# Who issues the four loads of block 0's A: ScalarE and SyncE, or SyncE alone

## The chip, the core and the metric

The kernel runs on one core of one Trainium2 chip. The metric is the device time of one execution in microseconds (us). The time before is the median of five runs, 474.98 us (474.37 to 475.48).

## The reference, cut to what matters

```python
# x (8, 256, 1024); A (8, 1024, 16); B (8, 16, 1024); one adapter number of 3..7 for each of 8 batches
Bx  = einsum('bni,bri->bnr', x, B[ids])          # rank 16
c   = einsum('bnr,bor->bno', Bx, A[ids])         # back to 1024
q   = fp8(clip(c / in_scale))                    # rounded to float8_e4m3
hid = silu(q @ gate_w.T) * (q @ up_w.T)          # 2752 wide, with scales
out = x + fp8(hid) @ down_w.T                    # with scales
```

So each batch picks a small adapter (B, then A) by its number, the result is rounded to fp8, and a feed-forward layer of 1024 to 2752 to 1024 follows, with x added at the end.

## The kernel before, in words

**Tiling.** The 8 batches of 256 tokens are four blocks (t = 0 to 3) of 512 tokens, two batches each. 1024 features are 8 slices of 128 (k). The 2752 hidden features are 22 slices of 128 (c), the last one half full. Everything is held transposed: features on partitions, tokens along the free dimension.

**Stages.** For block 0: `two_times_b` (L562) multiplies x by the two adapters' B into `bx`; VectorE and ScalarE copy it to `bm` (L578); `two_times_a` (L626) multiplies `bm` by A into `c`, 64 small products; VectorE and ScalarE round `c` to fp8 as `xg` (L614, L616). Then `gate_up(c, t)` (L686) makes 16 products of 128x512 for a slice c, and hid from them. The first `NFIRST` = 5 slices are done for block 0 alone (L762 to L771), then block 1's adapter stage (`two_times_b_in_parts`, `two_times_a_parts`) comes in the middle of slice 4, and so on to blocks 2 and 3. From slice 5 on, each weight tile serves all four blocks. Last come the products with the down weights (`yd`). A second path (`general`) is taken only for inputs that are out of bounds here; it does not run.

**Products of zeros.** `pass_time` (L527) issues products of a tile of zeros on TensorE at three places: 16 of 128x512 ahead of `two_times_b`, 4 of 128x128 between its k = 6 and k = 7, 7 of 128x128 between its end and `two_times_a` (L757 to L761). TensorE's order is written out by hand (`tc.keep_in_program_order`), so these stand where they stand whether data is there or not.

**Loads and their queues.** Nearly all loads are issued by SyncE, in program order, on one hardware queue (q1 in the profile). At the start ScalarE issues a few on its own queue (q10): the adapter numbers `ids_i`, the B of block 0's first batch, and two loads of block 0's A. A load of A or B needs its batch's adapter number in a register of the engine that issues it; `adapter_of` (L374) reads it there (`value_load`: a load from `ids_i`, register operations and a check, L375).

`a_two[0]` holds block 0's A as four groups of 16 rows. `load_a_two(t, j, adapter, queue)` (L382) loads the two groups g = 0, 1 of batch j, 32 KB each; the products of `two_times_a` read partitions 32q to 32q + 31, with q = 2g + j, in the order q = 0, 1, 2, 3. Thus "first" (j = 0) is read by q = 0 and 2, "second" (j = 1) by q = 1 and 3. The tile is filled with zeros by GpSimd before (L370).

The order of the loads at the start, as the program stands: x of block 0 in four pieces (k = 0-1, 2-4, 5-6, 7: 512, 768, 512 and 256 KB; L398), the two Bs (68 KB each; L378), the four As (L385), then the gate and up weights of slices 0 (two halves of 512 KB) and 1 to 4 (1 MB each; L408), six reads of adapter numbers, the Bs of block 1, x of block 1 in three pieces, its four As (`a_twice`, L391), x of block 2, and on.

**Eight completion semaphores.** The order of the built program shows that transfers take eight completion semaphores in turn, whichever engine issues them, and that an issue waits until the transfer that had its semaphore before has landed:

| semaphore | 0 | 1 | 2 | 3 | 4 | 5 | 6 | 7 |
|---|---|---|---|---|---|---|---|---|
| before, first turn | ids | x 0-1 | x 2-4 | B first | A first g0 (ScalarE) | A first g1 (ScalarE) | B second | x 5-6 |
| before, second turn | x 7 | A second g0 | A second g1 | w 0, half 0 | w 0, half 1 | w 1 | w 2 | w 3 |
| before, third turn | w 4 | B of block 1 | B of block 1 | x of block 1 | x of block 1 | x of block 1 | a_twice | a_twice |

So, for example, A second g1 waits for x 2-4, and w 1 waits for A first g1.

Of the kernel before, what the change touches and what calls it, by code (L numbers as in the profile page):

```python
# [284 lines left out]
def adaln_ffn(  # L285
# [15 lines left out]
    nc = tc.nc  # L301
# [48 lines left out]
    with ExitStack() as fast:  # L350
# [23 lines left out]
        def adapter_of(batch, queue):  # L374
            return queue.value_load(ids_i[0:1, batch : batch + 1], min_val=0, max_val=7)  # L375
# [6 lines left out]
        def load_a_two(t, j, adapter, queue=nc.sync):  # L382
            for g in range(2):
                row = 32 * (2 * g + j) + R * j
                queue.dma_start(  # L385
                    out=a_two[t][row : row + R],
                    in_=a8[bass.ds(adapter * 2 * R + g * R, R), :],
                )
# [6 lines left out]
        def load_x(t, k):  # L395
            piece, first = x_of(x4, t, k)
            ks = slice(first, first + piece.shape[1])
            nc.sync.dma_start(out=xs[t][:, ks, :], in_=piece)  # L398
# [16 lines left out]
        first, second = adapter_of(0, nc.scalar), adapter_of(1, nc.sync)  # L415
        load_b(b_two[0], 0, first, nc.scalar)
        load_b(b_two[0], 1, second, nc.sync)
        load_x(0, 5)
        load_a_two(0, 0, first, nc.scalar)
        load_x(0, 7)  # L420
        load_a_two(0, 1, second, nc.sync)
        for c in range(NFIRST):
            load_gate_up(c, parts=1 if c else 2)
        adapters = [adapter_of(2 + q, nc.sync) for q in range(6)]
# [434 lines left out]
        for k in range(NH - 1):  # L859
# [23 lines left out]
            first = k % 2 == 0  # L883
# [133 lines left out]
```

## Time and profile before

| | |
|---|---|
| median of five runs | 474.98 us |
| the profiled execution: time, span | 475.39 us, 473.6 us |
| TensorE busy | 468.6 us (99% of the span), 2482 products |
| VectorE, ScalarE, GpSimd busy | 107.0, 193.6, 11.5 us |
| DMA, mean over the span | 114 GB/s, 53.84 MB |
| DMA in the first 40 us | 370 GB/s, 14.78 MB |
| the two As issued by ScalarE | at 3.46 and 3.99 us, 3.9 and 4.8 us to landing |
| the two As issued by SyncE | at 4.51 and 6.06 us, 4.8 and 3.4 us to landing |

Times on a page of the profile count from the span's start. A row of the timeline is: start, duration from the first to the last end of the merged group, engine, line, operation, output<-inputs, count, and in brackets the idle time just before it with what ended it. PE is TensorE, PEld its weight loads, DVE VectorE, ACT ScalarE, POOL GpSimd; SPq and ACTq are the sequencers of SyncE and ScalarE, where a DMA_DIRECT2D is the issue of a transfer and not the transfer. The time to landing counts from the start of the issue. The chain of waits is followed back from the last instruction: at each step, what released it.

### The profile page before, as it was taken

Reading aid. Unit: us, or ns where it says so; the run is one execution under the profiler, and the core shown is the slowest. Engines: PE = TensorE matmul, PEld = TensorE weight load, DVE = VectorE, ACT = ScalarE, POOL = GpSimd, SP = SyncE. Lnnn points to the kernel's source line nnn. Section 1 sums busy time; section 2 is a strip of 40 time slices with the busy share of each in tenths; the row PEclk is TensorE's granted clock in tenths of the full one; section 3 lists DMA queues with packets and bytes.
Section 4 is the critical chain, followed back from the end, with each engine's and each line's share of the span. In section 5 each row is a group of like instructions: output and inputs, shape, how many; then the busy total and the mean of one; then the engine's idle time right before and its main releaser. Section 6 shows DMA issues by size and latency. Waiting matters only on the chain.

```text
span 473.6 us, 5982 instructions
## 1 busy us (share of the span) xinstructions
PE 468.6 (99%) x2482; PEld 215.8 (46%) x2482; DVE 107.0 (23%) x169; ACT 193.6 (41%) x253; POOL 11.5 (2%) x26
## 2 busy tenths in 40 slices
PE   9999999999999999999999999999999999999997
PEld 5444544444444444444444444444444444444444
DVE  1342621212122121212212121232120121031031
ACT  1342538995555645443354544359212022021000
POOL 0022300000000000000000000000000000000000
PEclk9999999999999999999999999999999999999999
DMA  8997023322222112222211111233335245163031
GB/s 312 412 381 220 1 88 120 148 90 89 90 89 90 61 34 84 89 90 89 90 62 35 37 62 57 61 101 106 110 141 161 71 179 162 28 215 108 3 115 68
DMA packets 15060, 53.84 MB, mean 114 GB/s; under 512 B 1778, under 2 KB 3058, under 8 KB 12978
## 3 DMA queue, kind: packets, MB, share of 16 engines
q1 hardware_dynamic: 14816, 53.25, 32.8%
q8 instruction: 21, 0.34, 0.3%
q10 hardware_dynamic: 210, 0.14, 0.1%
q14 instruction: 13, 0.11, 0.1%
HBM read 44.99 MB, written 8.39 MB: 113 GB/s over the span
## 4 chain that ended last, share of the span: by engine, by line
PE 92%; DMA 5%; ACT 0%; ACTq 0%; SPq 0%; DVE 0%; issue 0%; DVEq 0%
PE y L525 59%; PE yd L525 32%; DMA w_gu<-w_gu 3%; DMA a<-a_twice 2%; DMA a<-a 1%; PE c L525 1%; PE bx L525 1%; SPq L408 0%; ACT L310 0%; ACT xg L616 0%; ACTq L385 0%; ACTq L309 0%; ACTq L378 0%; DVE a_parts L454 0%; DVE a_parts L455 0%
## 5 line engine op out<-in xcount | busy, mean ns | idle before, releaser
L525 PE MATMUL y<-xg,w_gu 128*128 128x512 fp8e4 x1376 | 298.0, 379 | 0.2 <-ACT xg L616 0.2
L525 PEld LDWEIGHTS <-w_gu 128*128 128x128 bf16 x1376 | 134.2, 98 | 162.2 <-issue 0.6
L525 PE MATMUL yd<-hid,w_d 128*128 128x512 fp8e4 (+2 forms) x693 | 146.0, 373 | 0.0
L704 ACT ACTIVATE g<-y,gate_s 128x512 f32<-128x512 f32 (+1 forms) x88 | 59.7, 682 | 140.8 <-PE y L525 140.8
L733 DVE SCALAR_TENSOR_TENSOR hid<-y,up_by_down,g 128x512 fp8e4<-128x512 f32 x84 | 63.0, 751 | 217.2 <-PE y L525 154.0
L525 PEld LDWEIGHTS <-w_d 128*128 128x128 bf16 x693 | 66.6, 98 | 78.9 <-issue 1.7
L511 ACT ACTIVATE junk<-w_d 128x1408 bf16<-128x1408 uint16 (+1 forms) x16 | 21.2, 1323 | 88.3 <-DMA w_d<-w_d 88.2
L824 DVE SCALAR_TENSOR_TENSOR o<-yd,down_s,x 128x512 f32<-128x512 f32 x28 | 20.0, 746 | 107.5 <-PE yd L525 93.6
L511 ACT ACTIVATE junk<-w_gu 128x2048 bf16<-128x2048 uint16 (+1 forms) x22 | 41.0, 1863 | 0.0
L518 ACT ACTIVATE junk<-hid 128x2048 bf16<-128x2048 fp8e4 x21 | 40.0, 1906 | 0.5
L518 ACT ACTIVATE junk<-xg 128x2048 bf16<-128x2048 fp8e4 x8 | 15.3, 1909 | 0.3
L614 DVE TENSOR_SCALAR xg<-c,inv 128x512 fp8e4<-128x512 f32 (+1 forms) x17 | 11.0, 712 | 4.4 <-PE c L525 4.3
L616 ACT ACTIVATE xg<-c,inv 128x512 fp8e4<-128x512 f32 (+1 forms) x17 | 9.8, 664 | 2.3 <-PE c L525 2.3
L525 PE MATMUL warm<-zeros 128*128 128x512 bf16 (+1 forms) x27 | 7.1, 429 | 1.2 <-DVE zeros L312 1.2
L824 DVE SCALAR_TENSOR_TENSOR o<-yd,down_s,xg 128x512 f32<-128x512 f32 (+2 forms) x5 | 3.2, 644 | 12.3 <-PE yd L525 9.8
L525 PEld LDWEIGHTS <-zeros 128*128 128x128 bf16 x27 | 2.8, 123 | 5.1 <-issue 3.7
L511 ACT ACTIVATION_READ_ACCUMULATOR junk<-w_gu 128x1 f32 x22 | 4.2, 192 | 0.0
L525 PE MATMUL yd<-hid_tail,w_dt 64*128 64x512 bf16 (+1 forms) x32 | 4.1, 377 | 0.0
L733 DVE SCALAR_TENSOR_TENSOR tail<-y,up_by_down,g 64x512 fp8e4<-64x512 f32 x4 | 3.0, 756 | 4.9 <-ACT g L704 4.8
L518 ACT ACTIVATION_READ_ACCUMULATOR junk<-hid 128x1 f32 x21 | 3.9, 187 | 0.0
L525 PE MATMUL bx<-x,b_four_twice 128*32 128x256 f32 x64 | 3.7, 380 | 0.0
L578 ACT COPY bm<-bx 64x128 f32<-64x128 f32 x2 | 0.5, 262 | 7.2 <-PE bx L525 7.2
(69 smaller groups left out, 56.0 us busy)
## 6 DMA issues: line engine op xcount, KB each, us to landing
w_gu<-w_gu SPq DMA_DIRECT2D x13, 1024.0 KB, 4.8
w_gu<-w_gu SPq DMA_DIRECT2D x17, 512.0 KB, 4.1
outT<-o SPq DMA_DIRECT2D x31, 256.0 KB, 2.2
w_d<-w_d SPq DMA_DIRECT2D x8, 704.0 KB, 5.0
w_d<-w_d SPq DMA_DIRECT2D x8, 640.0 KB, 3.9
x<-x SPq DMA_DIRECT2D x2, 2048.0 KB, 12.4
x<-x SPq DMA_DIRECT2D x2, 768.0 KB, 9.2
x<-x SPq DMA_DIRECT2D x2, 512.0 KB, 4.0
```

The costliest lines, as they stand in the source:

```text
L511: nc.scalar.activation(junk_like(w), low(w), AF.Copy, accum_out=lows[:rows, column : column + 1])
L518: nc.scalar.activation(junk_like(q), q, AF.Square, accum_out=squares[:rows, column : column + 1])
L525: tc.keep_in_program_order(nc.tensor.matmul(*args, **kwargs))
L578: copy(bm[64 * to : 64 * (to + 1), other], bx[half][64 * half : 64 * (half + 1)],)
L614: nc.vector.tensor_scalar(to, c, scale, None, ALU.mult, saturate=False)
L616: nc.scalar.activation(to, c, AF.Copy, scale=scale, saturate=False)
L704: nc.scalar.activation(g[rows], gates, AF.Silu, scale=gate_s[: gates.shape[0]])
L733: nc.vector.scalar_tensor_tensor(to, in0=ups, scalar=up_by_down[rows], in1=g[rows], op0=ALU.mult, op1=ALU.mult, saturate=False,)
L824: nc.vector.scalar_tensor_tensor(o, in0=y, scalar=down_s, in1=x, op0=ALU.mult, op1=ALU.add)
```

## The change

```diff
         load_b(b_two[0], 0, first, nc.scalar)
         load_b(b_two[0], 1, second, nc.sync)
         load_x(0, 5)
-        load_a_two(0, 0, first, nc.scalar)
         load_x(0, 7)
-        load_a_two(0, 1, second, nc.sync)
+        load_a_two(0, 1, second)
+        load_a_two(0, 0, adapter_of(0, nc.sync))
         for c in range(NFIRST):
             load_gate_up(c, parts=1 if c else 2)
```

`load_a_two`'s default queue is SyncE's. ScalarE no longer issues any A. SyncE issues, behind the last piece of x (k = 7): A second g0, A second g1, a read of batch 0's adapter number into a register of SyncE's own, A first g0, A first g1; then the weights as before. ScalarE still reads the number of batch 0 for its load of B.

In the built program the order of the instructions on TensorE, VectorE, ScalarE and GpSimd is the same but for ScalarE's two issues. The semaphores of the first transfers change:

| semaphore | 0 | 1 | 2 | 3 | 4 | 5 | 6 | 7 |
|---|---|---|---|---|---|---|---|---|
| after, first turn | ids | x 0-1 | x 2-4 | B first | B second | x 5-6 | x 7 | A second g0 |
| after, second turn | A second g1 | A first g0 | A first g1 | w 0, half 0 | w 0, half 1 | w 1 | w 2 | w 3 |

From w 0 on, every transfer has the semaphore that it had before.

## The prediction

> **What bounds the kernel now.** I read the page's busy times and chain first, then the chain in order of time up to 57 us, then the timeline of the first 35 us, then the stretches of DMA.
>
> ```profile
> span 473.6 us, 5982 instructions
> PE 468.6 (99%) x2482; PEld 215.8 (46%) x2482; DVE 107.0 (23%) x169; ACT 193.6 (41%) x253; POOL 11.5 (2%) x26
> ...
> PE 92%; DMA 5%; ACT 0%; ACTq 0%; SPq 0%; DVE 0%; issue 0%; DVEq 0%
> ```
>
> TensorE is the bound nearly throughout. The 5% of DMA in the chain all stand in the first 32 us:
>
> ```profile
> 3.99 4.82 DMA a<-a
> ...
> 10.27 12.97 DMA w_gu<-w_gu
> ...
> 23.79 7.47 DMA a<-a_twice
> ...
> 31.35 0.29 DVE rest L600
> 31.67 0.48 DVE a_parts L454
> 32.17 0.43 DVE a_parts L455
> 32.61 0.14 issue
> 32.74 0.75 PE c L525 x16
> ```
>
> The first of these rows is one of the loads that the change moves. But the chain gets from it to the next only over SyncE's issues: weights 1 wait for that A's semaphore, and weights 4 are issued behind them. Whether that costs time depends on whether the DMA engines run out of work meanwhile. After 34.4 us the chain is TensorE alone. So the change can matter in two ways: through block 0's `c`, which needs all four As, or through the arrival of block 1's data at 30 to 31 us.
>
> ```profile
> 4.51 1.87 SPq L385 DMA_DIRECT2D a<-a  x2
> 6.43 4.29 SPq L408 DMA_DIRECT2D w_gu<-w_gu  x6
> 9.63 0.56 PE L525 MATMUL warm<-zeros 128*128 128x128 bf16 x7
> 9.73 0.60 DVE L578 COPY bm<-bx 64x128 f32<-64x128 f32 x2 [2.62 <-PE bx L525]
> 10.13 2.17 PE L525 MATMUL c<-bm,a 32*128 32x128 f32 x64
> 14.36 0.98 SPq L378 DMA_DIRECT2D b<-b  x2
> 29.45 1.23 PE L525 MATMUL bx<-x,b_twice 128*32 128x128 f32 x32 [0.48 <-DMA x<-x]
> 32.74 0.51 PE L525 MATMUL c<-bm_parts,a_parts 32*128 32x256 f32 x8 [0.23 <-DVE a_parts L455]
> ```
>
> Here one sees that `c` starts at 10.13 right behind the zeros (no idle time in its row), that the last A landed at 6.06 + 3.4 = 9.46, so 0.67 us earlier, and that TensorE has idle time only in block 1's stage: 0.48, then about 0.15 inside the group of 1.23 (its twin ahead of it took 1.08), then 0.23: 0.86 us together.
>
> **What the change does, part by part.**
>
> *ScalarE* loses two issues (3.46 to 4.32 us). Its next work is the copy to `bm` at 9.79, which waits for `bx`. Worth nothing: the wait of 7.22 us in front of that copy takes it all up.
>
> *SyncE* gets two issues and a read of a number. From the rows: x 7 is issued at 3.81 and A second g0 at 4.51, both as before (its old wait for x 0-1, landed at 0.73 + 3.3 = 4.03, was over). Two As in a row on ScalarE stand 0.53 us apart (3.46, 3.99), so A second g1 goes at 5.04 and ends at 5.38; its old wait for x 2-4 (to 6.06) is gone. The read costs 0.58: between the last issue of weights (6.43 + 4.29 = 10.72) and the issue at 14.36 stand six of them and 0.13 of register work. Then 0.19 of register work (0.53 less an issue of 0.34): A first g0 at 6.15, A first g1 at 6.68, both with their semaphores free (x 2-4 landed at 6.06). Weights 0, half 0, follow at 7.05 instead of 6.43: **0.62 us later**. Half 1 at 7.51 (7.41 before, as it waited for A first g0). Weights 1 wait for x 5-6, landed at 3.31 + 4.8 = 8.11, so 8.11 instead of 8.82; weights 2 to 4 follow about 0.3 to 0.7 earlier than their 9.19, 9.67 and 10.27, unless x 7 or the As hold them.
>
> *DMA.* Is there work while half 0 is 0.62 late? The stretches (span, busy engines, clock, share, GB/s):
>
> ```profile
> 0.00:2.00 2.00, 0.82 (x2) 0.28 (x3) 0.43 (x6) 0.71 (x1) 1.13 (x8) 1.00 0.17 25
> 2.00:4.00 2.00, 2.00 (x6) 0.76 (x5) 0.00 (x0) 0.57 (x1) 0.00 (x0) 1.00 0.90 354
> 4.00:6.00 2.00, 2.00 (x6) 0.76 (x5) 0.00 (x0) 0.00 (x0) 0.00 (x0) 1.00 1.02 380
> 6.00:7.00 1.00, 1.00 (x6) 0.34 (x4) 0.61 (x8) 0.00 (x0) 0.00 (x0) 1.00 1.03 366
> 7.00:8.00 1.00, 1.00 (x30) 0.72 (x32) 0.11 (x1) 0.00 (x0) 0.00 (x0) 1.00 1.00 363
> ```
>
> By 8.00 us 50 + 708 + 760 + 366 + 363 = 2247 thousand bytes had moved. Ahead of half 0 stand x (2048 KB), two Bs (136 KB) and four As (128 KB), 2312 KB or 2367 thousand bytes, the same in both kernels. So 120 thousand bytes are left at 8.00, 0.33 us at 363 GB/s: work until 8.33. The first x, issued at 0.73, shows its first bytes in the quarter from 1.50, some 0.9 us later (my estimate from those rows). Half 0 issued at 7.05 is thus there from about 7.95, 0.38 us before the queue runs dry. I price the late issue at nothing, covered by the queue of x and A. If the cover is gone, all later transfers shift by at most the 0.62, and with them block 1's data and the end: bounds 0 and 0.62. On the other side, earlier issues of weights can close the dip at 8 to 9 us (309 GB/s against 410 in the next microsecond, about 0.25 us), and no more. From then on the queue is full (a mean of 370 GB/s over 40 us) and serves the same bytes in the same order, whatever the issue times. I take 0, the nearest row being the queue itself.
>
> The Trainium skill ("DMA: Bandwidth & Descriptors", section "Issuing engines are not separate DMA queues") says that issuing from several engines saves only the sequencer's time, as all run on the same DMA engines. That speaks against this change by the sequencer's 0.62 us and by nothing else; taken as lost it would give the 0.62 above.
>
> *The As and `c`.* The last A is issued at 6.68 instead of 6.06. In the rows, SyncE's A of 4.51 landed at 9.31 and that of 6.06 at 9.46: 1.55 us between the issues, 0.15 between the landings. They land when the queue has come to them, behind x 7, not a fixed time after the issue. The bytes ahead are the same. Bounds: 6.68 + 3.4 = 10.08 by the shortest of the four rows, 6.68 + 4.8 = 11.48 by the longest; by the queue 9.46 to 9.6. I take 9.6, as the nearest row is an A behind the same x. `c` needs it at 10.13 (q = 2 is the third product): 0.5 us to spare, and even the shortest row's 10.08 is in time. No wait is added on the path. When the weights' half 0 lands later than its 6.43 + 4.1 = 10.53, by 0.62 at worst, that is 11.15, and `gate_up` reads it at 12.26.
>
> Sum against the profiled execution: 475.39 + 0 = 475.39. It lies 0.41 above the median of the five runs, so the forecast in terms of the median is **474.98, rounded 475.0**.
>
> **Rivals.**
>
> *A becomes the bound (slower).* The point is where the last A lands. Up to 10.13 nothing. Up to 10.13 + 0.86 = 10.99 TensorE's block 0 shifts, but block 1's stage waits for DMA anyway and gives it back. Beyond, it counts one to one: at the upper bound 11.48 about 0.5 us, 475.5. It would be slower by over 0.2% from a landing of 11.94, 5.3 us after the issue, longer than any of the four rows; or if the gap also slows TensorE. The first products of zeros have their weight loads 0.43 us apart from 1.58 to 6.28 (2.01, 2.44, 2.86), while 72 products of the same width at 12.26 take 15.7 us, 0.218 each: at the start TensorE runs at half speed for some 5.1 us. Falling back to that for as long would cost 2.55 us, so up to 478.1. Against it: after the idle 0.48 at 29 us the products keep their usual 379 ns. The skill ("TensorE: Matmul & The Clock Gate", section "Part 1: The HAM clock gate") puts the fall at an idle window of about 3.4 us; by that a gap of 1.3 us costs no clock.
>
> *The queue runs dry.* Half 0's first bytes come later than 8.33. For it: the dip to 309 GB/s shows that the queue was thin there. At most 0.62: 475.6, still within 0.2%.
>
> *Block 1's data comes earlier (faster).* By the dip, up to 0.25: 474.7. However early it came, TensorE can gain only its idle 0.86 (474.1), which is under 0.2%; more would need something that no row shows.
>
> *The change does not do what it says:* the order of the built program shows all four As on SyncE, so no chance is given.
>
> **How the numbers follow.** 0.2% (0.95 us) is about what a measurement of this kernel tells from no change. Hidden, at 475.0, own range 474.4 to 475.6: 0.72. Queue dry: 0.08, all within 0.2%. A bound: 0.13, of it 0.11 slower by over 0.2% and 0.02 within. Earlier data: 0.07, of it 0.04 faster and 0.03 within. So faster 0.04, same 0.85, slower 0.11. The range reaches from 474.2 (most of the idle 0.86 gained) to 476.0 (0.62 lost, and 0.4 for the profiled run's distance from the median).
>
> **What would show it.** Right: half 0 of the weights issued near 7.05 and weights 1 near 8.11; the last A landed by 10.1; `c` at 10.13 with no idle time; block 1's second `bx` group at 29.4 to 29.5; its `c` at 32.7 to 32.8. Wrong: idle time in front of `c`, products of `y` at 0.43 us apart behind it, a stretch under 250 GB/s between 8 and 9.5 us, or block 1's x landing off 30.2 by more than half a microsecond.

## The result and the profile after

| | before | after |
|---|---|---|
| median | 474.72 us (474.37 to 476.30, 47 runs) | 475.69 us (474.80 to 476.76, 27 runs) |
| ratio, 95% interval | | 1.0017 (1.0012 to 1.0022) |
| profiled execution, span | 475.39, 473.6 us | 476.09, 474.3 us |

The changed kernel is slower by 0.97 us by the medians, by 0.17% as a ratio. As a ratio that lies within the 0.2% of the forecast "same" (the 0.97 us of the medians is a hair above its 0.95), and 475.69 lies within the range of 474.2 to 476.0. But the change is clear of zero, and the forecast had put its cost at nothing. The 474.72 is the median of more runs of the kernel before than the five that gave 474.98.

The page after, with the same rows as before:

```profile
span 474.3 us, 5984 instructions
PE 468.1 (99%) x2482; PEld 215.9 (46%) x2482; DVE 107.0 (23%) x169; ACT 193.6 (41%) x253; POOL 11.5 (2%) x26
...
PE 92%; DMA 6%; SPq 1%; DVE 0%; issue 0%; ACT 0%; DVEq 0%
```

TensorE is busy for 0.5 us less in a span that is 0.7 us longer, so it waits about 1.2 us more. The chain has gained DMA time and issues of SyncE. In order of time, after:

```profile
3.81 4.72 DMA x<-x
...
9.76 13.84 DMA w_gu<-w_gu
...
24.15 7.82 DMA a<-a_twice
...
32.03 0.29 DVE rest L600
32.35 0.51 DVE a_parts L454
32.86 0.02 issue
32.89 0.44 DVE a_parts L455
33.32 0.14 issue
33.46 0.75 PE c L525 x15
```

No A of block 0 is in it any more, and the row that ends the DMA part, block 1's `c`, has moved from 32.74 to 33.46: the whole 0.7 us of the spans is there by 33.5 us. The timeline after:

```profile
4.46 2.57 SPq L385 DMA_DIRECT2D a<-a  x4
7.07 3.12 SPq L408 DMA_DIRECT2D w_gu<-w_gu  x6
9.02 0.56 PE L525 MATMUL warm<-zeros 128*128 128x128 bf16 x7
9.51 2.17 PE L525 MATMUL c<-bm,a 32*128 32x128 f32 x64
16.12 12.26 PE L525 MATMUL y<-xg,w_gu 128*128 128x512 fp8e4 x56 [0.86 <-DMA w_gu<-w_gu]
30.24 1.12 PE L525 MATMUL bx<-x,b_twice 128*32 128x128 f32 x32 [0.85 <-DMA x<-x]
33.46 0.51 PE L525 MATMUL c<-bm_parts,a_parts 32*128 32x256 f32 x8 [0.26 <-DVE a_parts L455]
```

SyncE did what was worked out: half 0 of the weights 0 at 7.07 (7.05 forecast). The last A, issued at 6.71, landed 2.5 us later at 9.2, ahead of `c` (9.51), which has no idle time. But `y` now waits for weights (slice 1), and `bx` of block 1 waits for x longer than before. The stretches of DMA after, to be laid beside 366, 363, 309, 410 GB/s before up to 10 us, and 397 from 10 to 12:

```profile
6.00:7.00 1.00, 1.00 (x20) 0.58 (x22) 0.61 (x8) 0.00 (x0) 0.00 (x0) 1.00 0.97 381
7.00:8.00 1.00, 1.00 (x41) 0.82 (x36) 0.11 (x1) 0.00 (x0) 0.00 (x0) 1.00 1.04 393
8.00:9.00 1.00, 1.00 (x28) 0.51 (x19) 0.00 (x0) 0.00 (x0) 0.00 (x0) 1.00 0.86 230
9.00:10.00 1.00, 1.00 (x25) 0.88 (x25) 0.57 (x2) 0.53 (x2) 0.00 (x0) 1.00 0.99 328
10.00:12.00 2.00, 2.00 (x62) 1.72 (x57) 1.26 (x2) 1.30 (x3) 0.00 (x0) 1.00 1.05 356
```

The rate falls at 8 us, with a busy share of 0.86 for 1.08 before, and it stays low until 14 us (381 GB/s from 12 to 14, for 414 before). (The clock column, 1.00, is full in both.)

### The profile page after: what moved, and what is told of

Read it like the earlier page. It is cut to its first block, busy times and chain, and to the rows that moved or that the text cites. A ratio compares the mean times of both kernels' runs of the same rounds, so it can differ in the third digit from the quotient of the medians.

```text
span 474.3 us, 5984 instructions
## 1 busy us (share of the span) xinstructions
PE 468.1 (99%) x2482; PEld 215.9 (46%) x2482; DVE 107.0 (23%) x169; ACT 193.6 (41%) x253; POOL 11.5 (2%) x26
## 4 chain that ended last, share of the span: by engine, by line
PE 92%; DMA 6%; SPq 1%; DVE 0%; issue 0%; ACT 0%; DVEq 0%
PE y L525 59%; PE yd L525 32%; DMA w_gu<-w_gu 3%; DMA a<-a_twice 2%; DMA x<-x 1%; PE c L525 1%; PE bx L525 1%; DMA ids_i<-ids 0%; SPq L408 0%; ACT xg L616 0%; SPq L375 0%; DVE a_parts L454 0%; SPq L398 0%; SPq L378 0%; DVE a_parts L455 0%
```

## The experiments

The theory after the result, called DRY: SyncE's later issue of half 0 starves the DMA engines, and block 1's data comes later by what was not moved. Its rivals, QUEUE (the As on one queue, or the changed turn of the semaphores) and CROWD (weights 1 to 4 issued earlier and closer together), share all symptoms in the profile above.

| run | median, us | before beside it | ratio (95%) | half 0 issued | mean GB/s, 6 to 14 us |
|---|---|---|---|---|---|
| e10, no read on SyncE | 474.72 | 474.68 | 0.9999 (0.9990 to 1.0007) | 6.46 | 393 |
| e3, two reads behind | 474.83 | 474.67 | 1.0002 (0.9993 to 1.0011) | 6.47 | 361 |
| e1, one read ahead | 475.54 | 474.67 | 1.0017 (1.0007 to 1.0026) | 7.06 | 353 |
| e2, two reads ahead | 476.01 | 474.67 | 1.0024 (1.0014 to 1.0033) | 7.75 | 324 |
| e8, half 0 by ScalarE | 475.55 | 474.68 | 1.0016 (1.0007 to 1.0025) | 6.12 | 386 |
| e5, half 0 before A first | 475.90 | 474.67 | 1.0029 (1.0016 to 1.0042) | 5.41 | 370 |
| e7, all As by ScalarE | 475.57 | 474.68 | 1.0016 (1.0005 to 1.0026) | 6.61 | 349 |
| e11, B second by ScalarE | 476.63 | 474.88 | 1.0033 (1.0021 to 1.0046) | 6.39 | 347 |

The last two columns are from one profiled execution each; in the same stretch four profiles of the two kernels unchanged show below what an execution varies by.

### The read alone, ahead of the weights (e1, e2) and behind them (e3)

```diff
+        adapter_of(1, nc.sync)          # e1: once; e2: twice
         for c in range(NFIRST):
             load_gate_up(c, parts=1 if c else 2)
+        adapter_of(1, nc.sync)          # e3: twice, here instead
```

All on the kernel before. Of the first:

> The kernel before, with one more read of an adapter number on SyncE (its result is not used) between the last A and the first half of the weights 0. All As stay where they were, two on ScalarE. Weights 0, half 0, should be issued near 7.0 us instead of 6.43, weights 1 at 8.8 as before. Theory DRY (the changed kernel loses its 0.7 to 0.9 us because SyncE issues half 0 some 0.6 us later, and the DMA engines run out of work between 8 and 9 us): as slow as the changed kernel, 0.5 to 0.9 us over before, a DMA stretch of 8.0 to 8.9 us near 214 GB/s instead of 326. Rival QUEUE (the As on one queue, or the changed turn of the semaphores, cost the time): no change, within 0.2 us of before. Rival CROWD (weights 1 to 4, issued 0.5 to 0.8 us earlier in the changed kernel and one right behind the other, slow the DMA engines between 9 and 14 us): no change either, since weights 1 to 4 go out as before.

> The same with two such reads: half 0 near 7.6 us. DRY: about 0.6 us more than with one read, 1.1 to 1.5 us over before, and the stretch without work longer by as much. QUEUE and CROWD: no change, within 0.3 us of before.

> The kernel before with the same two reads behind the weights 4 instead of ahead of the weights 0, beside the six reads that stand there. Control for the reads themselves: the transfers behind them are issued about 1.2 us later, but the DMA queue is then full. All theories: within 0.2 us of before. If it is slower by half a microsecond or more, reads on SyncE cost time for another reason than the late weights.

Measured: +0.87 us with one read, +1.34 with two, +0.16 (not clear of zero) with two behind. So a delay of half 0 alone, with the As untouched on their two queues and weights 1 issued at 8.83, costs what the change costs. QUEUE and CROWD both fail as the cause. One expectation of DRY failed, and it matters for the account below: e1's profile shows 311 GB/s between 8 and 9 us, as before (309), and falls short only later:

```profile
7.06 3.80 SPq L408 DMA_DIRECT2D w_gu<-w_gu  x6
```

```profile
8.00:9.00 1.00, 1.00 (x38) 0.80 (x31) 0.00 (x0) 0.00 (x0) 0.00 (x0) 1.00 1.13 311
9.00:10.00 1.00, 1.00 (x19) 0.66 (x17) 0.29 (x2) 0.26 (x1) 0.00 (x0) 1.00 1.07 336
10.00:12.00 2.00, 2.00 (x67) 1.93 (x64) 0.97 (x3) 1.00 (x3) 0.00 (x0) 1.00 0.98 379
12.00:14.00 2.00, 2.00 (x18) 0.94 (x12) 2.00 (x4) 1.68 (x3) 0.00 (x0) 1.00 0.96 348
```

The shortage is to be read over 6 to 14 us, not from one dip. e3's profiled execution took 477.11 us, the longest of its runs (474.49 to 477.11), so its 361 says nothing about the median. It does show that an execution can lose DMA rate, and time, without a late half 0.

### The change without its read (e10)

```diff
-        load_a_two(0, 0, adapter_of(0, nc.sync))
+        load_a_two(0, 0, second)
```

> The changed kernel without its read of batch 0's number on SyncE: A first is loaded with the number of the second batch, so that batch 0 is computed with the wrong A; the bytes, the queue, the two added issues and the turn of the semaphores are those of the changed kernel. SyncE is 0.58 us earlier: half 0 near 6.5 us, weights 1 to 4 still at 8.0 to 9.8. DRY: 474.5 to 475.0 us, the loss is gone but for 0.1 or so. QUEUE and CROWD: 475.4 to 476.0, as slow as the changed kernel.

Measured: 474.72 beside 474.68, no loss. The timeline of SyncE and TensorE in this kernel, then its DMA:

```profile
4.46 1.96 SPq L385 DMA_DIRECT2D a<-a  x4
6.46 3.54 SPq L408 DMA_DIRECT2D w_gu<-w_gu  x6
28.04 1.95 PE L525 MATMUL bx<-x,b_twice 128*32 128x128 f32 x64
32.03 0.51 PE L525 MATMUL c<-bm_parts,a_parts 32*128 32x256 f32 x8 [0.21 <-DVE a_parts L455]
```

```profile
6.00:14.00 8.00, 8.00 (x153) 5.37 (x152) 3.77 (x14) 2.95 (x6) 0.00 (x0) 1.00 1.03 393
```

All four As are on SyncE's queue, the semaphores have the changed turn, and weights 1 go out at 7.83, yet nothing is lost. The two added issues of A are free, because they fill the time in which SyncE had waited for the landing of x 2-4. Of the 0.64 us by which half 0 is late in the changed kernel, 0.6 are the read, and without it the loss is gone (to within -0.5 to +0.3 us, by the interval).

### Half 0 brought forward: two ways that met another bound (e5, e8)

In e5 half 0 goes out behind A second, ahead of the read and of A first; in e8 ScalarE issues it, after five reads that serve as a delay (the transfers of A, B and w are held in program order for it).

```diff
 # e5, on the changed kernel
-        load_a_two(0, 0, adapter_of(0, nc.sync))
-        for c in range(NFIRST):
-            load_gate_up(c, parts=1 if c else 2)
+        load_gate_up(0, 2, lambda: load_a_two(0, 0, adapter_of(0, nc.sync)))
+        for c in range(1, NFIRST):
+            load_gate_up(c)
 # e8, on the changed kernel
-        for c in range(NFIRST):
-            load_gate_up(c, parts=1 if c else 2)
+        for _ in range(5):
+            adapter_of(0, nc.scalar)
+        load_gate_up(0, 2, nc.scalar)
+        for c in range(1, NFIRST):
+            load_gate_up(c)
```

In e5 the lambda is called between the two halves of the weights 0; in e8 `nc.scalar` issues the first of them.

> The changed kernel, all four As on SyncE, with the first half of the weights 0 issued behind A second and ahead of the read and of A first: half 0 near 5.4 us, A first behind it, so that it lands near 10.4 us instead of 9.2, later than c could use it. DRY: the loss is gone, 474.5 to 475.0 us (0.2 under to 0.3 over before), no stretch under 280 GB/s between 8 and 9 us; the wait of c for A is given back in block 1's stage, where TensorE waits for DMA. QUEUE: as slow as the changed kernel or slower, 475.5 to 476.2, since the As are on one queue and late as well. CROWD: still slow, 475.4 to 475.9, since weights 1 to 4 go out early and one behind the other.

> The changed kernel, all four As on SyncE behind the read, in which ScalarE issues half 0 of the weights 0, behind the B of the first batch and five more reads that serve as a delay, so that it goes out near 6.2 us instead of 7.07. The As land as in the changed kernel, near 9.2 us. DRY: the loss is gone, 474.4 to 475.0 us, and the stretch of 8.0 to 8.9 us is above 280 GB/s again. QUEUE: as slow as the changed kernel, 475.4 to 476.0, since the As are still on SyncE's queue alone.

Measured: 475.90 and 475.55, not the 474.4 to 475.0 that DRY expected. e8's DMA is full (387 GB/s between 8 and 9 us, 386 over 6 to 14), so the shortage is cured; e5's moved to 9 to 10 us (234 GB/s). In neither does TensorE wait for weights or for x any more. It waits for A, the first row of e5, the second of e8:

```profile
11.02 2.36 PE L527 MATMUL c<-bm,a 32*128 32x128 f32 x64 [1.03 <-DMA a<-a]
```

```profile
10.81 2.24 PE L535 MATMUL c<-bm,a 32*128 32x128 f32 x64 [0.90 <-DMA a<-a]
```

That is the rival "A becomes the bound" of the prediction, which the change itself does not meet: an A that lands behind half 0, or beside it from the other queue, lands at 10.7 to 11.1 us. (e8's profile also loses 0.77 us ahead of block 1's `c`, as the second profile of before below does.) These two runs alone do not tell DRY from QUEUE by their times; e1 and e10 do.

### The mirror image, and a repaired version (e7, e11)

e7 lets ScalarE issue all four As. e11 keeps them on SyncE, puts both of SyncE's reads ahead of x 5-6, and gives the B of the second batch to ScalarE, so that SyncE pays for the read with an issue less.

```diff
 # e7, on the changed kernel
-        load_a_two(0, 1, second)
-        load_a_two(0, 0, adapter_of(0, nc.sync))
+        load_a_two(0, 0, first, nc.scalar)
+        load_a_two(0, 1, adapter_of(1, nc.scalar), nc.scalar)
 # e11, on the changed kernel
-        first, second = adapter_of(0, nc.scalar), adapter_of(1, nc.sync)
+        first = adapter_of(0, nc.scalar)
         load_b(b_two[0], 0, first, nc.scalar)
-        load_b(b_two[0], 1, second, nc.sync)
+        load_b(b_two[0], 1, adapter_of(1, nc.scalar), nc.scalar)
+        second, first = adapter_of(1, nc.sync), adapter_of(0, nc.sync)
         load_x(0, 5)
         load_x(0, 7)
         load_a_two(0, 1, second)
-        load_a_two(0, 0, adapter_of(0, nc.sync))
+        load_a_two(0, 0, first)
```

> The mirror image of the change: all four As issued by ScalarE, none by SyncE; ScalarE reads the number of the second batch too. SyncE has two issues less, but its x 7 then waits for the landing of x 2-4 (the turn of the semaphores), so that half 0 of the weights should go out near 6.5 us, about as before. DRY (the time follows the issue of half 0): within 0.3 us of before. QUEUE (what costs is that the As share SyncE's queue with x): as before or up to 0.5 us faster. So this run speaks mainly against a third view, that any move of an A costs.

> The changed kernel, all four As on SyncE, with the B of the second batch issued by ScalarE behind that of the first (after a read of its own), so that SyncE has an issue less and both its reads stand ahead of x 5-6. SyncE's added read is then paid by the issue that it lost: half 0 near 6.5 us. DRY: the loss is gone, 474.5 to 475.0 us, within 0.3 of before, and as many bytes moved between 6 and 14 us as before (3.1 MB; the changed kernel 2.7 to 2.9). If the B of the second batch, issued about 1.2 us later, lands after 7.0 us, bx may wait for it by up to 0.5 us; then up to 475.3. QUEUE: 475.4 to 476.0, since the As are on SyncE's queue alone.

Both missed: 475.57 and 476.63. In e7, x 7 waits for the landing of x 2-4 and goes out 2.4 us later than before; half 0 follows at 6.61 and weights 1, which wait for an A, at 8.55. The DMA rate falls to 307 GB/s between 7 and 8 us and to 279 between 9 and 10. That fits DRY in kind, with x 7 late as well, but no run separates the two. In e11 half 0 is early (6.39), but the B lands at about 9.1 us, later than feared, and half 1 has that B's semaphore and waits for it too:

```profile
9.16 1.73 PE L526 MATMUL bx<-x,b 128*32 128x128 f32 x54 [2.37 <-DMA b<-b]
```

So no version here beats the kernel before. e10 has its time, but it leaves out the read of batch 0's number and uses the second batch's A for it.

### Which execution was usual (four more profiles)

> The kernel before, unchanged, for another profile: the profiled execution of before took 475.39 us against a median of 474.7 over many runs, so it may not be the usual one. If the usual execution has less waiting for DMA in block 1's stage, then block 1's c starts at 32.0 to 32.3 us (32.74 in the first profile), TensorE's idle time there is 0.2 to 0.4 us instead of 0.86, and so the change has less idle time in which to lose its delay. Rival: the idle time of 0.86 is usual, and the 0.7 us above the median stand elsewhere, before 10 or after 35 us.

> As the look before this one, a second execution of the kernel before.

> The changed kernel, unchanged, for another profile. Theory DRY: TensorE waits for DMA again in block 1's stage, 0.8 to 1.2 us there and around slice 1, block 1's c starts at 32.9 to 33.5 us, and 8.0 to 8.9 us has under 260 GB/s.

> As the look before this one, a second execution of the changed kernel.

Times 474.43 and 475.38 before, 476.83 and 475.96 after. Over 6 to 14 us the three profiles of before moved 384, 396 and 395 GB/s, the three of after 351, 338 and 358. The means differ by 43 GB/s over 8 us, 340 thousand bytes, or 0.83 us at 410 GB/s: the size of the loss. Two expectations missed: between 8.0 and 8.9 us the two profiles of after show 287 and 285 GB/s, not under 260, and `c` of block 1 lies outside the expected times in three of the four. The first new profile of before, close to the median:

```profile
27.78 2.04 PE L525 MATMUL bx<-x,b_twice 128*32 128x128 f32 x64
29.75 1.90 PE L525 MATMUL y<-xg,w_gu 128*128 128x512 fp8e4 x8
31.83 0.51 PE L525 MATMUL c<-bm_parts,a_parts 32*128 32x256 f32 x8 [0.18 <-DVE a_parts L455]
```

Here `bx` of block 1 is one group of 64 without a wait for x, and `c` starts at 31.83. The second profile has no wait for x either; its `c` starts at 32.77, after 0.80 us of waiting for VectorE's `a_parts`. What goes with it can be read from the rows of that operation, which VectorE and GpSimd each do on a part of A. First the profile close to the median, then the second:

```profile
31.26 0.43 DVE L455 TENSOR_TENSOR a_parts<-a,a_parts 128x256 fp32r<-128x256 f32 x1
31.62 0.73 POOL L455 TENSOR_TENSOR a_parts<-a,a_parts 128x256 fp32r<-128x256 f32 x1
```

```profile
31.62 0.72 POOL L455 TENSOR_TENSOR a_parts<-a,a_parts 128x256 fp32r<-128x256 f32 x1
31.72 0.91 DVE L455 TENSOR_TENSOR a_parts<-a,a_parts 128x256 fp32r<-128x256 f32 x1
```

VectorE's takes 0.91 us in the two profiles in which GpSimd's began 0.1 us before it (this one and e8), and 0.42 or 0.43 in the twelve others; no run tells why.

So the 0.48 of waiting for x stands in one of three profiles of before, and not in the one close to the median: there x of block 1 is in time, and a later arrival finds little to hide in. After, `c` starts at 34.17 and 33.36, with waits for weights (0.56, 0.82) and, in one of the two, for x (1.31). In 13 of the 14 profiles, of whatever version, the time less the start of block 1's `c` is 442.60 to 442.66 us (442.82 in e3): all that a version gains or loses is settled by then.

## Why the prediction was right in its range and wrong in its mechanism

- **SyncE's timing: right.** Half 0 at 7.07 for 7.05, 0.64 late for 0.62. The read is 0.6 of it. That weights 1 to 4 go out earlier and gain nothing was right as well.
- **The cover of the late issue: right for the first bytes, and too little.** It was priced "at nothing, covered by the queue of x and A": half 0 "there from about 7.95", against a queue that lasts until 8.33. The trace holds every DMA packet, and half 0's are known by their 4 KB. The first of them starts at 8.13, 8.20 and 8.17 us in the three profiles after, at 8.28, 8.16 and 8.23 before, at 8.26 in e1, and in each the last packets of x or A start later than that. So the queue as a whole did not run empty, though the engines' busy share from 8 to 9 us fell to 0.86, 0.92 and 0.99, for 1.08 to 1.10 before. Half 0 starts slowly after: its first 16 packets took 330, 210 and 360 ns in the median, for 185, 201 and 183 before, 159 in e10 and 212 in e1. The rates from 6 to 11 us after, in steps of 0.125 us, show what that makes:

```profile
GB/s 398 393 360 393 328 426 426 328 393 393 377 377 426 377 410 394 197 131 328 164 98 197 295 426 295 295 295 295 328 393 328 393 361 328 262 328 328 426 360 393
```

  The rate falls from 394 to 197 at 8.0 us and is below 200 in five of the six steps from there. The same is seen at the very start of before, in steps of 0.25 us from 1 us on (x issued at 0.73):

```profile
GB/s 0 0 33 164 82 295 393 311 442 426 467 418 418 442 344 418 418 257 333 411 400 361 377 328 369 353 426 303 279 369 328 262 426 360 442 410 360 377 377 393
```

  First bytes at 1.50, but 295 only at 2.25 and 393 at 2.50, so 1.5 to 1.8 us after the issue. Counted so, half 0 is at the full rate at 8.6 to 8.8, after the 8.33. The row was read for its first nonzero number instead of its first full one.
- **The queue from then on: the step that failed.** "From then on the queue is full [...] and serves the same bytes in the same order, whatever the issue times. I take 0". It serves them more slowly. The mean GB/s by stretch:

| us | before, three profiles | after, three profiles | e1 | e10 |
|---|---|---|---|---|
| 8 to 9 | 316 | 266 | 311 | 373 |
| 9 to 10 | 407 | 318 | 336 | 397 |
| 10 to 12 | 418 | 336 | 379 | 389 |
| 12 to 14 | 421 | 384 | 348 | 422 |

  Of the 377 thousand bytes that are missing after 8 us, only 50 thousand are missing between 8 and 9; the rest is lost from 9 to 14 us, though weights 1 to 3 (3 MB) had all been issued by 9.4 us. e1 shows it most plainly: its first bytes were covered as the prediction had reckoned, its rate between 8 and 9 us is that of before, and it lost 0.87 us. The engines were hardly idle: over 8 to 14 us their busy share is 0.93 to 1.01 after and 1.05 or 1.06 before. Packets took longer: of the 389 to 460 of 2 to 8 KB that start in these 6 us, 24, 17 and 34 took over twice the usual time of their size (159 ns for 4 KB, 309 for 8 KB) after, 15 in e1 and 32 in e2, but 4, 0 and 0 before and 3 in e10. That a late half 0 brings the loss about is shown by the times of e1, e2 and e10; why the packets then take longer is open. That early weights 1 to 4 crowd the engines is excluded by e10, and no run tried anything else.
- **The bound on that step: too small.** At most 0.62 was to be lost; 0.97 by the medians, 0.8 by the ratio was.
- **The idle time that would take up a delay: wrong place to read it.** The 0.86 us came from an execution that lay 0.67 above the later median; in the two later profiles of before, the waits for x in it were gone. That it was one execution was said, but only used to shift the forecast.
- **A and `c`: right.** Landed at 9.2, no wait. The rival "A becomes the bound" did not happen in the change, and its mechanism was shown by e5 and e8, where A lands at 10.7 to 11.1 and `c` waits 0.9 to 1.0.
- **The skill's rule.** The Trainium skill ("DMA: Bandwidth & Descriptors", section "Issuing engines are not separate DMA queues") says that several issuers save only sequencer time, usually small beside the transfer. The runs agree: taking the read away gave the loss back (e10), one queue or two made no difference there, and 0.6 us is small beside the 4.1 us in which half 0 lands. But these 0.6 us of sequencer time cost 0.8 to 1.0 us of the end.
- **"Queue dry"** was on the list of rivals, at 0.08 and 475.6. In size it comes nearest, and its sign, a stretch under 250 GB/s between 8 and 9.5 us, is there in the first profile after (230). Its condition, first bytes later than 8.33, is not.
- **The range held by luck.** 475.69 lies outside the 474.4 to 475.6 of the case that was forecast. It lies within 476.0 because 0.4 us had been added there for the distance of one profiled execution from the median, which has nothing to do with the loss.

## What to carry to other kernels

When an issuing engine gets one more instruction ahead of a stream of transfers, that the next transfer's first byte comes before the queue is empty does not make the delay free: here it did come in time, and the rate was low for 5 us more. Put the instruction alone into the old kernel at that place, as in e1, and measure what it costs. A register read on the issuer can cost more than the transfers that it serves: here two more issues were free, as they filled a wait, and without the read of about 0.6 us no loss was left. Slack read from one profiled execution should be looked at in a second one that is close to the median before it is spent.

## What the runs showed of the hardware that was not expected

- The products of zeros at the start go from 0.43 us apart to half of that at different times: in the first profile of before the slow spacing lasts until 6.28 us, after until 4.57, with the same instructions. So `c` of block 0 starts at 9.51, 9.85 and 10.43 us in three executions of the changed kernel, and the last A, landed at 9.2, 9.6 and 9.6, has 0.3, 0.2 and 0.8 us to spare.
- In the changed kernel the As issued by SyncE at 6.18 and 6.71 landed 2.9 and 2.5 us after their issue; in e8, where half 0 came from the other queue at 6.12, the A issued at 6.34 took 4.3 us. What stood ahead of it on its own queue was the same; new was the half 0 beside it on the other queue, with which it shared the engines.
- Where two transfers share a completion semaphore, the later waits for the earlier one's landing before it is issued. In e11 a late B so held back weights that have nothing to do with it: 164, 33 and 0 GB/s in three steps of 0.125 us from 9.75 us on.
